# A Macaron block on one core: the first layer's expert rows added into three sums in HBM instead of two

## The chip, the core and the metric

The kernel runs on one core of one Trainium2 chip. The metric is device time in microseconds (us) from launch to end. A kernel's time here is the median of its runs. One further execution was taken with the hardware profiler, and all views of a profile come from that one.

Engines are called as in the profile: PE is TensorE's matmuls, PEld its weight loads, DVE is VectorE, ACT is ScalarE, POOL is GpSimd, SP is SyncE. SP computes nothing here; it issues DMAs. POOL, besides the constants at the start, issues the DMAs that gather, scatter or add.

## What is computed

The input is 4 sequences of 512 rows of 512 numbers, all float32. Three steps follow one another:

```
x = x + 0.5 * ffn(layernorm(x))
x = x + attention(layernorm(x))
x = x + 0.5 * ffn(layernorm(x))
```

`ffn` is a mixture of experts plus a shared expert. Each of the 2048 rows chooses 6 of 64 experts; an expert takes the rows that chose it, at most 96 of them, and computes `(silu(x @ w_gate) * (x @ w_up)) @ w_down` with a hidden size of 192. Its results, times the row's weight for that expert, are added to the row:

```
h = silu(einsum('ech,ehf->ecf', buf, w_gate)) * einsum('ech,ehf->ecf', buf, w_up)
out = einsum('ecf,efh->ech', h, w_down)
y = segment_sum(out[expert, slot] * w, token) + shared_expert(x)
```

So six expert results have to be added to each row, in float32. The two ffn steps use the same weights. The attention has 16 heads of 32, with rotary embedding.

## The kernel before, in words

**Stages.** From 0 to about 164 us the first layer's routing runs (row norms, choice of experts, lists of rows per expert), with the shared expert for three of the four sequences between its steps. From 164 to 458 us the first layer's expert loop runs (`experts(0, ...)`), then the attention for the four sequences in turn, whose pieces also do the second layer's routing. At about 1178 us the last sequence's routing follows, from 1229 us the second layer's expert loop, and at the end 16 DMAs add one sum to the output (line 1171).

**The expert loop** (`experts`, lines 531 to 608) goes over 32 pairs of experts. For pair n PE runs, in this order: the transposes of pair n+1's gathered rows (`turn`, line 547), the gate and up products of pair n (`hidden`, line 562, 96 matmul records), the down products of pair n-1 (`down`, line 577, 12 records). PE's order is written out by hand throughout.

- The rows of an expert are gathered by an indirect DMA that POOL issues (`load_rows`, line 538), into one of 11 buffers `xr`. A buffer is free again when the expert's results have been scaled, since the scale is read from it.
- The weights of a pair are three DMAs of 768 KB that SP issues (lines 262 to 264). There are six places for pairs, so those of pair n+6 go into the place of pair n once that is used up.
- The results of an expert stand in one of four PSUM banks (`eo`, pool psD). ACT scales them into a buffer `ob` (line 581; four buffers), and POOL issues an indirect DMA that adds its 96 rows into a sum in HBM (line 582). This is a scatter-add.
- Within the first layer, even experts add into `total[0][0]` and odd ones into `total[0][1]`. Two scatter-adds into the same sum may meet in a row, so each waits until the one before it into the same sum has landed. `total[0][0]` begins as the rows plus the shared expert's part (stored at line 528; for sequence 3, whose rows stay in SBUF, as zeros), `total[0][1]` as zeros (`clear`, line 235).

**From the loop to the attention.** In PSUM the loop's pools lie thus: psA, for the loop's turns, on banks 0 and 1; psB, for `gu`, on banks 2 and 3; psD, for `eo`, on banks 4 to 7. The attention opens psS (three tiles of two banks, banks 0 to 5) and then psT (banks 6 and 7). PE first runs the shared expert for the last sequence (lines 1068 to 1075), whose products go to psS tiles by the class `Banks`, and whose turns go to psT. Meanwhile the sums come back (`load`, line 614). For the first sequence SP loads the row tile of `total[0][0]` and that of `total[0][1]` (called `odd`), and DVE adds the two (line 808). For sequences 1 and 2 SP loads the one and POOL adds the other by an accumulating DMA (line 627). For sequence 3, which is in SBUF already, POOL adds both. The rows of sequence 1 are first read by the row statistics that DVE takes while the first sequence's projections run (`summed(1)`, line 1085; line 170). DVE's and ACT's orders are written out by hand here; POOL's and SP's orders are chosen by a scheduler when the program is made.

**The first 50 us.** SP's order is written out by hand: 16 loads of input rows (line 661) and three of shared weights, then for each of nine steps the store of the normed rows (line 309), read later by the gathers. `xn` has two buffers, so ACT's line 307 waits for the store two steps back.

Of the kernel before, what the change touches and what calls it, by code (L numbers as in the profile page):

```python
# [9 lines left out]
F32 = mybir.dt.float32  # L10
# [7 lines left out]
P = 128  # L18
B, S, D = 4, 512, 512
# [12 lines left out]
CAP = 96  # L32
# [51 lines left out]
def macaron_kernel(ctx: ExitStack, tc: tile.TileContext, X, ln_w, ln_b, W_in, W_out, gate_w, bias,  # L84
# [125 lines left out]
    def gate_up(bT, weights, rows, psum, pool, bufs):  # L210
# [8 lines left out]
        def products():  # L219
# [6 lines left out]

    xn_d = [dram.tile([T + P, XW], F32, tag=f"xn_d{i}", name=f"xn_d{i}") for i in range(2)]
    total = [[dram.tile([T + P, D], F32, tag=f"total{i}{j}", name=f"total{i}{j}") if (i, j) != (1, 0) else out  # L230
              for j in range(2)] for i in range(2)]

    def clear(layer, tiles):

# [31 lines left out]
    def load_now(*args):  # L266
        for go in load_pair(*args):
            go()
# [262 lines left out]
    def experts(layer, en, extra, psA, psB, psD, also):  # L531
        with ExitStack() as s:
            ep = s.enter_context(tc.tile_pool(name=f"ep{layer}", bufs=2))
            rows = {}

            def load_rows(e):
                xr = ep.tile([CAP, XW], F32, tag="xr", name="xr", bufs=GA + 5)
                nc.gpsimd.indirect_dma_start(  # L538
                    out=xr, out_offset=None, in_=xn_d[layer],
                    in_offset=bass.IndirectOffsetOnAxis(ap=en[:, e:e + 1], axis=0))  # L540
                rows[e] = xr

            bTs, hTs = {}, {}

            def turn(e):
                bTs[e] = ep.tile([P, DC, CAP], F32, tag="bT", name="bT", bufs=4)
                transposed(bTs[e], rows[e], DC, P, CAP, psA, nc.vector.tensor_copy)

            def hidden(n):


                wg, wu, _ = loaded[layer, n]
                xa, xb = bTs.pop(2 * n), bTs.pop(2 * n + 1)
                both = []
                for w in (wg, wu):
                    ps = psB.tile([P, 512], F32, tag="ps", name="gu")
                    both.append(ps[:, :3 * CAP])
                    g = both[-1].rearrange("p (k r) -> p k r", k=3)
                    for k in range(3):
                        for c in range(DC):  # L560
                            for t, x in enumerate((xa, xb)):
                                nc.tensor.matmul(g[t * FT:(t + 1) * FT, k, :], lhsT=w[:, t, c, k::3], rhs=x[:, c, :],  # L562
                                                 start=c == 0, stop=c == DC - 1)
                sg = ep.tile([P, 3 * CAP], F32, tag="sg", name="sg")
                hT = ep.tile([P, 3, CAP], F32, tag="hT", name="hT")
                nc.scalar.activation(sg, both[0], AF.Tanh, scale=0.5)  # L566
                nc.vector.scalar_tensor_tensor(sg, sg, 1.0, both[0], ALU.add, ALU.mult)  # L567
                nc.vector.tensor_mul(hT.rearrange("p k r -> p (k r)"), sg, both[1])
                hTs[n] = hT

            def down(n):
                wd, hT = loaded.pop((layer, n))[2], hTs.pop(n)
                eos = [psD.tile([P, 512], F32, tag="ps", name="eo") for _ in range(2)]
                for c in range(3):
                    for k in range(2):
                        r = slice(k * FT, (k + 1) * FT)
                        nc.tensor.matmul(eos[k][:CAP], lhsT=hT[r, c, :], rhs=wd[r, c, :], start=c == 0, stop=c == 2)  # L577
                for k in range(2):
                    e = 2 * n + k
                    ob = ep.tile([CAP, D], F32, tag="ob", name="ob", bufs=4)  # L580
                    nc.scalar.activation(ob, eos[k][:CAP], AF.Copy, scale=rows.pop(e)[:, D + e:D + e + 1])  # L581
                    nc.gpsimd.indirect_dma_start(  # L582
                        out=total[layer][k], in_=ob, in_offset=None,
                        out_offset=bass.IndirectOffsetOnAxis(ap=en[:, e:e + 1], axis=0),
                        compute_op=ALU.add, **(dict(bounds_check=T - 1, oob_is_err=False) if layer and not k else {}))

            for e in range(GA):
                load_rows(e)
            turn(0)
            turn(1)  # L590
            for n in range(E // 2 + 1):
                for e in range(2 * n + GA, min(2 * n + GA + 2, E)):
                    load_rows(e)
                if n + 1 < E // 2:
                    turn(2 * n + 2)
                    turn(2 * n + 3)
                if n < E // 2:
                    hidden(n)
                    if n + WS + WX + 1 < E // 2:
                        *gates, below = load_pair(layer, n + WS + WX + 1, extra)  # L600
                        for go in gates:
                            go()
                if n > 0:
                    down(n - 1)
                    for go in lasts:
                        go()
                lasts = [below] if n + WS + WX + 1 < E // 2 else []
                also(n)
# [5 lines left out]
    def load(b, i, op=None):  # L614

        rows = slice((b * TPB + i) * P, (b * TPB + i + 1) * P)
        if b < B - 1:
            x = row_tile(b * TPB + i)
            nc.sync.dma_start(x, total[0][0][rows, :])
            xas.setdefault(b, []).append(x)  # L620
        x = xas[b][i]
        if b == 0:
            odd = op.tile([P, 2, S], F32, tag="pT", name="odd")[:, 0, :]
            nc.sync.dma_start(odd, total[0][1][rows, :])
            return odd
        for k in range(1 if b < B - 1 else 0, 2):
            nc.gpsimd.dma_start(x, total[0][k][rows, :], accum_op=ALU.add, max_dma_last_dim=D)

    win, chunks = [], []
# [19 lines left out]
    with ExitStack() as s:  # L649
# [4 lines left out]
        with ExitStack() as f:  # L654
# [19 lines left out]
            for t in range(2 * TPB + 1):  # L674
                g, i = divmod(t, TPB)
                if t == TPB - 1:
                    with tc.issue_after(route.begun):
                        route.begin(1, xs[1])
                if g < 2:
                    route.row(g, xs[g], i)  # L680
                    route.turn(g, i)
                if t > 0:
                    route.score(*divmod(t - 1, TPB))
                if t == TPB:
                    for later in range(2, B):
                        with tc.issue_after(route.begun):
                            route.begin(later, xs[later])
                    route.choose(0)
# [61 lines left out]
    with ExitStack() as s:  # L750
# [2 lines left out]
        vp = s.enter_context(tc.tile_pool(name="vp", bufs=2))  # L753
        ap = s.enter_context(tc.tile_pool(name="ap", bufs=2))
        rp = s.enter_context(tc.tile_pool(name="rp1", bufs=1))
        psS = s.enter_context(tc.tile_pool(name="psS", bufs=3, space=bass.MemoryType.PSUM))
        psT = s.enter_context(tc.tile_pool(name="psT", bufs=2, space=bass.MemoryType.PSUM))
        s.enter_context(tc.manual_schedule(engines={mybir.EngineType.Activation, mybir.EngineType.DVE}))
        route = Route(1)
        route.use(rp, psT, psT, 2)  # L760
# [41 lines left out]
        def qkv(b):  # L802
# [2 lines left out]

            def row(i):
                if b == 0:
                    nc.vector.tensor_add(xs[b][i], xs[b][i], odds.pop(0))
                    if i + 2 < TPB:
                        odds.append(load(0, i + 2, op))  # L810
                    if i == 1:
                        load_win(3)
                        for later in range(1, B):
                            for k in range(TPB):
                                load(later, k)
                    for _ in first(b, row_stats(xs[b][i:i + 1]), (i,)):
                        pass
                while (b, i) not in stats:
                    work.flush(1)
                m, rr, _, _ = stats[b, i]  # L820
                lns[i] = ap.tile([P, D], F32, tag="row", name="ln", bufs=1)
                nc.vector.scalar_tensor_tensor(lns[i], xs[b][i], m, lnw_b, ALU.subtract, ALU.mult)
                nc.vector.scalar_tensor_tensor(lns[i], lns[i], rr, lnb_b, ALU.mult, ALU.add)
# [302 lines left out]
    with ExitStack() as s:  # L1126
        extra = s.enter_context(tc.tile_pool(name="wx1", bufs=WX))
        for n in range(WS, WS + WX):
            load_now(1, n, extra)
        psA = s.enter_context(tc.tile_pool(name="psA1", bufs=2, space=bass.MemoryType.PSUM))  # L1130
        psB = s.enter_context(tc.tile_pool(name="psB1", bufs=2, space=bass.MemoryType.PSUM))
        psD = s.enter_context(tc.tile_pool(name="psD1", bufs=4, space=bass.MemoryType.PSUM))
        with ExitStack() as f:
            g = B - 1
# [75 lines left out]
```

## Time and profile before

| what | us |
|---|---|
| median of 3 runs | 1554.72 (1552.41 to 1554.78) |
| time of the profiled execution | 1552.3 |
| its span, first to last instruction | 1550.6 |
| first gather of the first loop issued | 150.1 |
| first `hidden` matmul, pair 0 | 164.5 |
| the same, pair 31 | 434.4 |
| last scatter-add of the first loop issued | 457.3 |
| first `hidden` matmul of the second loop | 1229.5 |

| engine | busy us, share of the span |
|---|---|
| PE | 1358.0 (88%) |
| PEld | 774.0 (50%) |
| DVE | 628.8 (41%) |
| ACT | 596.9 (38%) |
| POOL | 350.7 (23%) |

How to read it: the chain of waits starts at the last instruction and goes back, at each step, to what released it. A line such as "DMA total<-ob,en" in it is a scatter-add that somebody waited for. "issue" is time for which the profile shows no reason. A line of the list of instructions ends, in square brackets, with the idle time of the engine before it and what ended that. A row of a stretch's busy times has the granted TensorE clock (1.00 is full speed), the busy share of the DMA engines and the bytes that they moved. That share adds up the packets of all queues, which overlap, so that it can exceed 1. Engine totals mix stages with different limits; what a change in one stage is worth has to be read in that stage.

### The profile page before, as it was taken

The page shows a single profiled execution, that of the slowest core. Times are in us where ns is not written, and L with a number is a line of the kernel's source. Part 1 is how long each engine was busy: PE and PEld are TensorE (multiplying, and loading weights), DVE is VectorE, ACT ScalarE, POOL GpSimd, SP SyncE. Part 2 cuts the span into 40 slices and gives each one's busy share as a digit, 9 for nine tenths or more (in the row PEclk, how much of TensorE's full clock was granted, in tenths as well). Part 3 has the DMA queues.
Part 4 walks back from the last instruction along what each step waited for, and adds up shares of the span by engine and source line. Part 5 has one row for each costly group of instructions (what it writes and reads, how often), then busy time and mean ns, then how long its engine had stood idle before and what let it go on. Part 6 is the DMA issues. An engine that isn't in the chain of part 4 may idle for free.

```text
span 1550.6 us, 27673 instructions
## 1 busy us (share of the span) xinstructions
PE 1358.0 (88%) x11328; PEld 774.0 (50%) x11328; DVE 628.8 (41%) x1572; ACT 596.9 (38%) x1161; POOL 350.7 (23%) x321
## 2 busy tenths in 40 slices
PE   4785899988978998999999999998898899989890
PEld 4553676766643443334443334334344577766660
DVE  7575222221216576257333862375515522222210
ACT  4431121211111377667645785557462121111120
POOL 2001455554435000000000000000000255555455
PEclk9898899999989997999899999996998999999995
DMA  5367999999979210000000001000205699999959
GB/s 198 133 229 264 313 322 323 323 328 336 327 210 184 63 68 1 1 1 0 21 21 18 1 16 74 11 14 34 92 1 209 198 335 332 337 332 322 331 127 124
DMA packets 110717, 254.86 MB, mean 164 GB/s; under 512 B 15848, under 2 KB 32360, under 8 KB 110592
## 3 DMA queue, kind: packets, MB, share of 16 engines
q1 hardware_dynamic: 70880, 192.96, 35.4%
q0 software_dynamic: 39424, 59.97, 18.8%
q8 instruction: 90, 1.47, 0.4%
q14 instruction: 35, 0.29, 0.1%
q10 hardware_dynamic: 288, 0.16, 0.0%
HBM read 202.21 MB, written 56.95 MB: 167 GB/s over the span
## 4 chain that ended last, share of the span: by engine, by line
PE 42%; DMA 30%; issue 7%; ACT 5%; DVE 4%; POOL 2%; SPq 0%; POOLq 0%; ACTq 0%; DVEq 0%
DMA total<-ob,en 19%; PE pq L834 10%; DMA out_dram<-ob,en 9%; PE sct L1018 5%; PE sc L988 4%; PE cx L1041 4%; PE sct L1022 4%; PE po L883 3%; PE gu L214 3%; PE so L520 3%; DMA xr<-xn_d,en 2%; PE ps_t L207 2%; ACT sc L996 2%; PE lg L320 1%; POOL out_dram L1171 1%
## 5 line engine op out<-in xcount | busy, mean ns | idle before, releaser
L538 POOL DMA_INDIRECT xr<-xn_d,en x128 | 119.6, 934 | 883.6 <-DVE sg L221 711.8
L562 PE MATMUL gu<-bT,w 128*64 128x96 f32 x6144 | 296.9, 258 | 0.0
L562 PEld LDWEIGHTS gu<-bT,w 128*64 128x64 f32 x6144 | 286.4, 175 | 8.7 <-issue 1.8
L581 ACT ACTIVATE ob<-eo,xr 96x512 f32<-96x512 f32 x128 | 85.7, 682 | 409.8 <-PE eo L577 187.6
L996 ACT ACTIVATE sc<-sc,nmq 128x512 f32<-128x512 f32 x256 | 168.9, 660 | 56.0 <-DVE nmq L991 50.4
L834 PE MATMUL pq<-w,lT 128*128 128x512 f32 x384 | 179.3, 614 | 6.2 <-ACT lT L208 2.7
L991 DVE TENSOR_REDUCE nmq<-sc 128x2 f32<-128x1024 f32 x128 | 151.5, 1221 | 76.1 <-PE sc L988 76.0
L582 POOL DMA_INDIRECT total<-ob,en x96 | 138.5, 1443 | 186.2 <-DMA total<-ob,en 143.6
L577 PE MATMUL eo<-w,hT 64*96 64x512 f32 x768 | 180.0, 602 | 0.0
L208 DVE COPY bT<-ps_t 128x384 f32<-128x384 f32 x128 | 68.6, 555 | 209.6 <-PE ps_t L207 209.6
L1029 ACT ACTIVATE pT<-sct 128x1024 f32<-128x1024 f32 x128 | 124.1, 1022 | 61.8 <-PE sct L1022 61.8
L834 PEld LDWEIGHTS pq<-w,lT 128*128 128x128 f32 x384 | 71.5, 195 | 96.8 <-issue 81.0
L207 PE MATMUL ps_t<-ident,xr 96*128 96x96 f32 x512 | 64.2, 258 | 56.7 <-DMA xr<-xn_d,en 39.4
L214 PE MATMUL gu<-wsgu,xT 128*128 128x384 f32 x256 | 97.2, 528 | 8.4 <-ACT ob L581 8.1
L567 DVE SCALAR_TENSOR_TENSOR sg<-sg,gu 128x288 f32<-128x288 f32 x64 | 29.1, 455 | 181.6 <-ACT sg L566 181.6
L207 PEld LDWEIGHTS ps_t<-ident,xr 96*128 96x128 f32 x512 | 46.8, 143 | 109.1 <-issue 80.7
L988 PE MATMUL sc<-kT,qT 32*128 32x512 f32 x512 | 94.6, 706 | 7.0 <-ACT sc L996 6.3
L1018 PE MATMUL sct<-qT,kT 32*128 32x512 f32 x512 | 94.6, 661 | 2.8 <-ACT pT L1029 2.7
L577 PEld LDWEIGHTS eo<-w,hT 64*96 64x96 f32 x768 | 58.7, 159 | 74.1 <-issue 68.3
L1022 PE MATMUL sct<-nmT,pick 4*128 4x512 f32 x512 | 86.7, 604 | 0.0
L214 PEld LDWEIGHTS gu<-wsgu,xT 128*128 128x128 f32 x256 | 52.0, 209 | 50.5 <-issue 18.3
L1041 PE MATMUL cx<-pT,v 128*32 128x512 f32 x512 | 73.5, 630 | 0.5 <-DVE acc L470 0.5
(163 smaller groups left out, 1317.5 us busy)
## 6 DMA issues: line engine op xcount, KB each, us to landing
w<-in_L_ffn_w_gate_dram SPq DMA_DIRECT2D x64, 768.0 KB, 21.4
w<-in_L_ffn_w_up_dram SPq DMA_DIRECT2D x64, 768.0 KB, 21.8
w<-in_L_ffn_w_down_dram SPq DMA_DIRECT2D x64, 768.0 KB, 21.6
total<-zero SPq DMA_DIRECT2D x39, 256.0 KB, 4.7
xn_d<-xn SPq DMA_DIRECT2D x32, 256.0 KB, 2.0
out_dram<-total POOLq DMA_DIRECT2D x16, 256.0 KB, 10.9
x<-total POOLq DMA_DIRECT2D x11, 256.0 KB, 10.2
shelf<-in_L_attn_X_dram SPq DMA_DIRECT2D x9, 256.0 KB, 7.2
```

Of the source, the lines that this page charges most:

```text
L207: nc.tensor.transpose(view[:, c, :], src[:, c * w:(c + 1) * w], ident[:rows, :rows])
L214: nc.tensor.matmul(gu[:rows, :2 * F].rearrange("p (w f) -> p w f", w=2), lhsT=bT[:, c, :], rhs=weights[:, :, c, :], start=c == 0, stop=c = ...
L562: nc.tensor.matmul(g[t * FT:(t + 1) * FT, k, :], lhsT=w[:, t, c, k::3], rhs=x[:, c, :], start=c == 0, stop=c == DC - 1)
L577: nc.tensor.matmul(eos[k][:CAP], lhsT=hT[r, c, :], rhs=wd[r, c, :], start=c == 0, stop=c == 2)
L582: nc.gpsimd.indirect_dma_start(out=total[layer][k], in_=ob, in_offset=None, out_offset=bass.IndirectOffsetOnAxis(ap=en[:, e:e + 1], axis=0 ...
L834: nc.tensor.matmul(pq, lhsT=lTs[i][:, c, :], rhs=win[n][c], start=c == 0, stop=c == DC - 1)
L988: nc.tensor.matmul(scs[j // 2][:, j % 2, :], lhsT=qT[b][rows, c, q * P:(q + 1) * P], rhs=kT[b][rows, c, :], start=True, stop=True)
L991: nc.vector.tensor_reduce(nmv[:, q, 2 * pair:2 * pair + 2, c], scs[pair], AX.X, ALU.max, negate=True)
L996: nc.scalar.activation(scs[j // 2][:, j % 2, :], scs[j // 2][:, j % 2, :], AF.Exp, bias=nmq[:, q, j * DH + c:j * DH + c + 1], accum_out=sm ...
L1018: nc.tensor.matmul(scs[j // 2][:, j % 2, :], lhsT=kT[b][rows, c, kt * P:(kt + 1) * P], rhs=qT[b][rows, c, :], start=True, stop=False)
L1022: nc.tensor.matmul(scs[j // 2][:, j % 2, :], lhsT=pick[rows, c, :], rhs=nmT[b][c // (NC - 1)][rows, :], start=False, stop=True)
L1041: nc.tensor.matmul(cx[c][j * DH:(j + 1) * DH, :], lhsT=v[b][:, kt, h * DH:(h + 1) * DH], rhs=pTs[j // 2][:, j % 2, :], start=kt == 0, stop ...
```

## The change

1. The first layer's scatter-adds go into three sums by `e % 3`. A third tensor `total[0][2]` is cleared by 17 DMAs of 256 KB, two in each of the nine steps at the start, ahead of the step's store of normed rows.
2. Reading back: for the first sequence SP loads two `odd` tiles for each row tile and DVE adds twice; for the others POOL issues one more accumulating DMA for each row tile.
3. `ob` has five buffers instead of four, in both layers' loops.
4. The attention's psT is opened ahead of psS, so it takes banks 0 and 1, and psS banks 2 to 7. In the last stage psB1 is opened ahead of psA1.

```
     total = [[dram.tile([T + P, D], F32, tag=f"total{i}{j}", name=f"total{i}{j}") if (i, j) != (1, 0) else out
-              for j in range(2)] for i in range(2)]
+              for j in range(3 - i)] for i in range(2)]
...
-                    ob = ep.tile([CAP, D], F32, tag="ob", name="ob", bufs=4)
+                    ob = ep.tile([CAP, D], F32, tag="ob", name="ob", bufs=5)
                     nc.scalar.activation(ob, eos[k][:CAP], AF.Copy, scale=rows.pop(e)[:, D + e:D + e + 1])
                     nc.gpsimd.indirect_dma_start(
-                        out=total[layer][k], in_=ob, in_offset=None,
+                        out=total[layer][e % (3 - layer)], in_=ob, in_offset=None,
...
-            odd = op.tile([P, 2, S], F32, tag="pT", name="odd")[:, 0, :]
-            nc.sync.dma_start(odd, total[0][1][rows, :])
+            odd = op.tile([P, 2, S], F32, tag="pT", name="odd")
+            for k in (1, 2):
+                nc.sync.dma_start(odd[:, k - 1, :], total[0][k][rows, :])
             return odd
-        for k in range(1 if b < B - 1 else 0, 2):
+        for k in range(1 if b < B - 1 else 0, 3):
             nc.gpsimd.dma_start(x, total[0][k][rows, :], accum_op=ALU.add, max_dma_last_dim=D)
...
+                for k in range(2 * t, min(2 * t + 2, NT + 1)):
+                    nc.sync.dma_start(total[0][2][k * P:(k + 1) * P, :], zero[:, :D])
                 if g < 2:
                     route.row(g, xs[g], i)
...
+        psT = s.enter_context(tc.tile_pool(name="psT", bufs=2, space=bass.MemoryType.PSUM))
         psS = s.enter_context(tc.tile_pool(name="psS", bufs=3, space=bass.MemoryType.PSUM))
-        psT = s.enter_context(tc.tile_pool(name="psT", bufs=2, space=bass.MemoryType.PSUM))
...
-                    nc.vector.tensor_add(xs[b][i], xs[b][i], odds.pop(0))
+                    odd = odds.pop(0)
+                    for k in range(2):
+                        nc.vector.tensor_add(xs[b][i], xs[b][i], odd[:, k, :])
...
+        psB = s.enter_context(tc.tile_pool(name="psB1", bufs=2, space=bass.MemoryType.PSUM))
         psA = s.enter_context(tc.tile_pool(name="psA1", bufs=2, space=bass.MemoryType.PSUM))
-        psB = s.enter_context(tc.tile_pool(name="psB1", bufs=2, space=bass.MemoryType.PSUM))
```

## The prediction

> **What bounds the kernel now.** I read the page first, the chain that ended last above all, then the chain over the first expert loop, the sums by stretch around its end, the instructions there in order of time, and the read-back of the sums.
>
> ```profile
> PE 42%; DMA 30%; issue 7%; ACT 5%; DVE 4%; POOL 2%; SPq 0%; POOLq 0%; ACTq 0%; DVEq 0%
> DMA total<-ob,en 19%; PE pq L834 10%; DMA out_dram<-ob,en 9%; PE sct L1018 5%; PE sc L988 4%; PE cx L1041 4%; PE sct L1022 4%; PE po L883 3%; PE gu L214 3%; PE so L520 3%; DMA xr<-xn_d,en 2%; PE ps_t L207 2%; ACT sc L996 2%; PE lg L320 1%; POOL out_dram L1171 1%
> ```
>
> The largest item is the scatter-add. The same chain over part of the first loop, in order of time:
>
> ```profile
> 268.58 0.52 issue
> 269.10 0.02 POOLq L538
> 269.12 0.19 issue
> 269.31 8.32 DMA total<-ob,en
> 277.63 0.02 issue
> ```
>
> One scatter-add into a sum lands after 8.3 us, 0.8 us go by, and the next into that sum is issued: 9.1 to 9.2 us for each pair, since each sum gets one expert of a pair. PE would need 8.0: pairs 1 to 8, before the four `ob` buffers are used up, start 8.0 us apart (171.1 to 227.1 us). Pairs 8 to 31 start on average 9.0 apart (227.1 to 434.4). The end of the loop, by stretch and by instruction:
>
> ```profile
> core 0: us, PE busy (x) PEld busy (x) DVE busy (x) ACT busy (x) POOL busy (x), PEclk, DMA share, GB/s
> 187.00:440.00 253.00, 234.64 (x3344) 174.29 (x3344) 55.45 (x112) 48.69 (x87) 127.26 (x106) 0.99 1.05 328
> 445.00:452.00 7.00, 0.00 (x0) 0.00 (x0) 0.00 (x0) 1.66 (x3) 2.81 (x2) 0.68 0.50 68
> 452.00:460.00 8.00, 7.56 (x15) 4.21 (x16) 0.71 (x2) 0.72 (x2) 4.21 (x3) 0.64 0.59 73
> ```
>
> ```profile
> 451.71 0.68 ACT L581 ACTIVATE ob<-eo,xr 96x512 f32<-96x512 f32 x1 [3.06 <-DMA total<-ob,en]
> 452.44 8.05 PE L214 MATMUL gu<-wsgu,xT 128*128 128x384 f32 x16 [8.09 <-ACT ob L581]
> ...
> 468.67 2.75 PE L214 MATMUL gu<-wsgu,xT 128*128 128x384 f32 x8
> ...
> 474.94 0.68 DVE L808 TENSOR_TENSOR shelf<-shelf,odd 128x512 f32<-128x512 f32 x1
> ...
> 480.27 0.75 DVE L823 SCALAR_TENSOR_TENSOR ln<-ln,rs,lnb_b 128x512 f32<-128x512 f32 x1
> ```
>
> PE's last `eo` ends at 444.36. It then stands for 8.09 us: the next matmul needs PSUM that the last `ob` (451.71 to 452.39) frees, and that one waited for a scatter-add to free its buffer. Then 16 matmuls take 8.05 us where 8 later take 2.75. DMA is close to full through the loop (328 GB/s, share 1.05), a second limit just behind the first.
>
> **The third sum and the fifth buffer.** With three sums, an expert's scatter-add waits for the one three before: 3 in 9.2 us, 6.1 us for a pair, under PE's 8.0. This holds only if a landing stays near 8.3 us with more in flight. The page "DMA: Bandwidth & Descriptors" of the Trainium skill (section "Anatomy of one DMA") speaks against it: a fixed cost of about 2.0 us, mostly the receipt of the last write, the rest data movement. By that, some 6 of the 8.3 us would be occupied DMA engines, and a third scatter-add in flight would only lengthen the queue; the loop would gain nothing. The packets in the trace decide: 96 of 2048 bytes belong to each scatter-add, and put to the issues in order they start 5.1 us after the issue and go on until 7.1, for nearly every one from pair 10 to 25. Landing follows about 1 us later. So only 2.0 of 8.3 us are movement; the rest is delay that overlaps. I take the trace. The gathers' packets take 1.6 us of the same queue, so a pair needs 2 x 2.0 + 2 x 1.6 = 7.2 us of it, which fits into 8.0, though narrowly.
>
> Next late are the weights. SP's queue works in order, so counting its bytes tells when each load was in: the up weights of pair 12 at 232.5, used at 262.4; of pair 20 at 314.7, used at 334.8; of pair 31 at 423.3, used at 434.4. The lead shrinks from 29.9 to 11.1 us. A faster loop uses it up and then runs at the pace of the loads, whatever PE could do. Earlier scatter-adds also come in the loads' way: in half microseconds full of scatter packets SP's queue moved 193 GB/s, without any from POOL's queue 339. One costs the loads 2.0 x (339 - 193) / 339 = 0.86 us. At 423 us the scatter-adds up to pair 26 were through; PE at the loads' heels needs about 6 more by then: 5.2 us. So pair 31's weights come at 428.5, and its first matmul moves from 434.4 to there: **-5.9**. (Bounds: -11.1 if the extra traffic costs nothing; 0 if it costs the whole lead.)
>
> From there PE has 9.9 us of matmuls (434.44 to 444.36). Then only the two last `ob` remain, as after pair 0, whose second ended 1.3 us after its `eo`. With five buffers the last `ob` needs the scatter-add five before, issued some 10 us earlier. The stop of 8.1 us becomes 1.3: **-6.8** (0 if a wait for a landing stays).
>
> The short stop should also save the slow start. "TensorE: Matmul & The Clock Gate" (Part 1) says an idle window of about 3.4 us halves the clock. Here 0.68 and 0.64 were granted over 445 to 460, and the 16 matmuls cost 8.05 - 2 x 2.65 = 2.75 us more than at full clock. After 1.3 us idle I count this as gone: **-2.7** (0 if the clock drops anyway).
>
> **The fifth buffer in the second loop: 0.** It is paced by its two sums as before (8.0 to 8.7 us landings in its chain), whatever waits ahead of them. Bounds: -4 (an expert's pace) to +1.
>
> **The changed banks: 0.** PE's first matmul after the loop writes bank 0, yet waits for the last `ob`, whose bank is 6: a pool waits for all of every pool it overlaps. psS on banks 2 to 7 overlaps psD as it did on 0 to 5, and the first matmul is still in psS. In the last stage the scores come up to 1.7 us sooner (they waited for DVE L885), but the next ones wait for DVE's statistics of the last row. Bounds: -1.5 to +0.5.
>
> **Clearing the third sum.** 17 DMAs of 256 KB at the start; over 20 to 60 us the DMA share is below a third, which hides 15 of them. The first two pairs stand in SP's queue ahead of the first two stores of `xn`, whose first landing (22.07) already ends a 1.9 us wait of ACT L307. Two more DMAs at 0.65 us, the pace of SP's issues there: **+1.3**, on PE's row of transposes and scores. Bounds: 0 to +3.
>
> **Reading back.** DVE's second add is 0.68 us for each of four rows. The first lies on the path (L808 to L823 to PE); the fourth as well, since PE waits for its `ln` at 518.43; the two others have over 4 us of slack: **+1.4**. The eight SP loads instead of four (0.43 us to issue) lie under the shared expert's 25 us of PE work, with the rows needed 12 us after the last landing; without that cover they would cost about 3 us.
>
> POOL issues 28 accumulating DMAs instead of 16:
>
> ```profile
> L627 POOL DMA_DIRECT2D x<-total x11: 1268/1847/5985, 465.9 to 503.2; - x11
> L627 POOL DMA_DIRECT2D shelf<-total x5: 1283/2373/3497, 470.9 to 479.3; - x5
>   DMA x<-total: 13.8, 3
>   DMA shelf<-total: 3.7, 1
> ```
>
> The 16 took from 466 to about 508, 2.65 us each; 28 will take 75. The second add to a row waits for the first (median landing 8.8), and POOL's later DMAs queue behind that wait. DVE reads sequence 1's rows (L170) at 503.9 to 509.7, where their adds landed by about 490. Everything shifts by some 13 us, so the reads come at 491 to 497, and POOL can start at about 453. If sequence 1's eight adds are among the first 14, they land by 453 + 14 x 2.65 = 490: no cost. If spread to the 20th place, 506: 9 us of DVE standing still, and behind it the rotary products and PE. I take **+2**, near the first, since POOL's present order puts sequence 1 in places 2 and 4 to 6. Bounds 0 and +9. Sequences 2 and 3 are read at 617 and later: hidden.
>
> **Sum.** -5.9 - 6.8 - 2.7 + 1.3 + 1.4 + 2 = -10.7. Against the profiled 1552.3 (span 1550.6 and 1.7 around it) that gives 1541.6. The runs' median, 1554.72, lies 2.4 above the profiled time; from it 1544.0.
>
> **Rivals.**
> *The weights' queue is the whole bound* (0.15): pair 31 stays at 434.4 and only the tail gains: -6.8 - 2.7 + 4.7 = -4.8, 1550. For it: 1.05 and 328 GB/s throughout. Against: 11.1 us of lead left.
> *The third sum only queues* (0.07): a landing grows to 3 x 9.2 / 2 = 13.8 us, pace and stop stay, and the added work remains: +3 to +5, 1558. For it: POOL's queue would be full for 7.2 of 8.0 us. Against: the packets.
> *The rows of sequence 1 come late* (0.16), the case that ends slower: POOL's order takes the adds of all rows once before second ones. If sequence 1's last is in place n, it lands at 453 + 2.65 n, against 497. The other terms gain 12.7, so it decides from n = 22 on; at n = 24 the wait is 20 us: +7, 1562. For it: the adds take turns on the DMA engines anyway. Against: the present order.
> *The change does not do what it says*: for the banks I assume just that (0 above). If the pool's wait were for its own banks only, 1.3 us more would be gained.
>
> **How the numbers follow.** The likeliest case (0.62) gives 1544, by itself 1537 to 1551. A change within 0.2% (3.1 us), about what a measurement of this kernel can tell from none, needs terms of two cases at their ends. Faster: the likeliest case nearly whole and most of the second: 0.73. Slower: the third and most of the fourth: 0.17. Within: 0.10. Range 1536 to 1559: at its low end the loads cost nothing extra and the adds are in time, at its high end the adds are late.
>
> **What would show it.** Right: in the first loop ACT no longer waits for landings before `ob`; three scatter-adds are in flight, landing in 8 to 10 us; pair 31 starts at 426 to 431, now behind its weights; PE's stop after the loop is under 2 us and L214's first 16 matmuls take about 5.4. Wrong: landings of 12 us or more, or a long DVE wait at L170 for POOL's adds between 490 and 520.

## The result, and the profile after

The changed kernel takes 1558.92 us (median of 22 runs, 1552.51 to 1569.77), the kernel before in the same series 1554.62 (22 runs, 1546.55 to 1564.64): ratio 1.0040, 95% interval 1.0023 to 1.0058. It is 0.4% slower; the forecast was 1544.0 us, 0.7% faster. The profiled execution took 1555.39 us, with a span of 1553.7. That 1558.9 still lies inside the stated range of 1536 to 1559 is luck: the range's high end was meant for rows of sequence 1 that come late, and they did not.

The chain of waits of the changed kernel, by engine and by line:

```profile
PE 48%; DMA 9%; ACT 5%; DVE 4%; issue 3%; POOL 1%; POOLq 0%; DVEq 0%; ACTq 0%
PE pq L840 10%; DMA out_dram<-ob,en 8%; PE sct L1024 5%; PE gu L563 5%; PE sc L994 4%; PE cx L1047 4%; PE sct L1028 4%; PE po L889 3%; PE gu L214 3%; PE ps_t L207 3%; PE so L521 3%; PE eo L578 2%; ACT sc L1002 2%; PE lg L321 1%; DMA xr<-xn_d,en 1%
```

The scatter-adds of the first layer, 19% of the chain before, are gone from it, and PE's own gate and up products (`gu L563`) are in it instead. What ScalarE waited for in the first loop, before (187 to 453 us) and changed (187 to 450 us); columns are total, times, longest, in us:

```profile
ACT ob L581 <- DMA total<-ob,en: 90.7, 29, 5.7
```

```profile
ACT ob L582 <- PE eo L578: 144.4, 29, 5.2
```

So the third sum does what it says: no scaled rows wait for a landing any more. The stretches of the first loop and of its end in the changed kernel, and PE's and ACT's instructions at that end:

```profile
187.00:440.00 253.00, 242.94 (x3352) 178.43 (x3350) 54.97 (x114) 47.65 (x86) 132.72 (x111) 1.00 1.05 329
445.00:452.00 7.00, 5.61 (x25) 2.26 (x22) 0.00 (x0) 2.51 (x4) 3.77 (x3) 1.00 1.04 291
```

```profile
449.24 1.26 ACT L582 ACTIVATE ob<-eo,xr 96x512 f32<-96x512 f32 x2 [1.32 <-issue]
```

```profile
450.55 5.43 PE L214 MATMUL gu<-wsgu,xT 128*128 128x384 f32 x16 [1.39 <-ACT ob L582]
```

The stop behind the loop is 1.39 us (8.09 before), and its 16 matmuls take 5.43 us (8.05 before), as forecast. Yet the loop holds 242.94 us of PE work for 3352 matmuls where it held 234.64 for 3344: they take longer. Where the two profiles differ (us; the experiments show below that they come from two kinds of chip):

| stretch | before | changed | difference |
|---|---|---|---|
| start to pair 0's first matmul | 164.5 | 170.9 | +6.4 |
| from there to pair 31's | 269.9 | 268.4 | -1.5 |
| pair 31 to the last `eo` | 9.9 | 9.8 | -0.1 |
| stop behind the loop | 8.1 | 1.4 | -6.7 |
| from there to attention's first projection | 30.0 | 28.8 | -1.2 |
| to the second loop's first gather | 733.8 | 737.7 | +3.9 |
| to pair 32's first matmul | 13.2 | 15.4 | +2.2 |
| to the end | 321.1 | 321.2 | +0.1 |

**The start.** ScalarE's instructions in the changed kernel, then in the kernel before (start, duration, what):

```profile
30.58 1.26 ACT L308 ACTIVATE xn<-shelf,off,rs 128x512 f32<-128x512 f32 x1
33.04 0.58 ACT L208 COPY xT<-ps_t 128x512 f32<-128x512 f32 x1 [1.20 <-PE ps_t L207]
34.64 0.22 ACT L326 ACTIVATE lgs<-lg 128x64 f32<-128x64 f32 x1 [1.01 <-PE lg L321]
34.76 1.28 ACT L308 ACTIVATE xn<-shelf,off,rs 128x512 f32<-128x512 f32 x1
```

```profile
28.83 1.26 ACT L307 ACTIVATE xn<-shelf,off,rs 128x512 f32<-128x512 f32 x1
29.89 0.62 ACT L208 COPY xT<-ps_t 128x512 f32<-128x512 f32 x1
31.16 0.22 ACT L325 ACTIVATE lgs<-lg 128x64 f32<-128x64 f32 x1 [0.64 <-PE lg L320]
32.01 0.59 ACT L208 COPY xT<-ps_t 128x512 f32<-128x512 f32 x1 [0.63 <-PE ps_t L207]
33.61 0.23 ACT L325 ACTIVATE lgs<-lg 128x64 f32<-128x64 f32 x1 [1.01 <-PE lg L320]
33.73 2.31 ACT L307 ACTIVATE xn<-shelf,off,rs 128x512 f32<-128x512 f32 x2
```

Before, a row is normed (`xn`) ahead of the copies of the row before it. In the changed kernel each row goes alone: norm, transpose, copy, score, then the next norm, 4.2 us a row, and PE waits for each `xn`. Nothing wrote this order by hand: here only SP's and PE's orders are, and the scheduler that makes the program (the planner, in what follows) places ACT's and DVE's instructions. The waits of ACT for a store of normed rows, from 20 to 46 us, before and changed:

```profile
ACT xn L307 <- DMA xn_d<-xn: 1.9, 1, 1.9
```

```profile
ACT xn L308 <- DMA xn_d<-xn: 3.2, 1, 3.2
```

The zeros in front of the stores thus cost ACT the 1.3 us that were forecast; the rest of its delay is not a wait for a store. The tenth row is stored at 50.33 us instead of 43.37, the first weights are asked for at 69.91 instead of 63.83.

**The loop.** PE and then POOL in pair 14 of the changed kernel:

```profile
290.90 4.54 PE L563 MATMUL gu<-bT,w 128*64 128x96 f32 x91
295.66 0.51 PE L563 MATMUL gu<-bT,w 128*64 128x96 f32 x5 [0.22 <-issue]
```

```profile
291.20 1.45 POOL L583 DMA_INDIRECT total<-ob,en  x1 [3.11 <-ACT ob L582]
292.95 0.94 POOL L539 DMA_INDIRECT xr<-xn_d,en  x1 [0.30 <-issue]
294.19 1.45 POOL L583 DMA_INDIRECT total<-ob,en  x1 [0.30 <-DMA total<-ob,en]
```

Of 96 matmuls, 91 have begun when PE starts no other for some 0.5 us (0.22 of it without any running); it goes on at 295.66, where POOL's third issue ends (295.64). Pairs 2 to 28 nearly all have this, at the same place against POOL. It is POOL's place that counts, not PE's: in pair 10 POOL's issues stand some 0.36 us earlier in the block, and PE stops after 84 matmuls instead of 91:

```profile
255.81 4.12 PE L563 MATMUL gu<-bT,w 128*64 128x96 f32 x84
260.20 0.82 PE L563 MATMUL gu<-bT,w 128*64 128x96 f32 x12 [0.28 <-issue]
```

```profile
258.74 1.45 POOL L583 DMA_INDIRECT total<-ob,en  x1 [0.30 <-issue]
```

Nor do the loads of the program's own instructions explain it: they come about once a pair too, but end anywhere from 0.1 to 5.3 us from the stop. The blocks of pairs 2 to 28 last 5.2 us instead of 4.50 and pairs start 8.7 to 8.8 us apart instead of 8.0.

### The profile page after: what moved, and what is told of

It is laid out like the page before. It is cut to its first block, busy times and chain, and to the rows that moved or that the text cites. A ratio compares the mean times of both kernels' runs of the same rounds, so it can differ in the third digit from the quotient of the medians.

```text
span 1553.7 us, 27718 instructions
## 1 busy us (share of the span) xinstructions
PE 1366.2 (88%) x11328; PEld 777.1 (50%) x11328; DVE 630.1 (41%) x1576; ACT 594.7 (38%) x1161; POOL 365.8 (24%) x333
## 4 chain that ended last, share of the span: by engine, by line
PE 48%; DMA 9%; ACT 5%; DVE 4%; issue 3%; POOL 1%; POOLq 0%; DVEq 0%; ACTq 0%
PE pq L840 10%; DMA out_dram<-ob,en 8%; PE sct L1024 5%; PE gu L563 5%; PE sc L994 4%; PE cx L1047 4%; PE sct L1028 4%; PE po L889 3%; PE gu L214 3%; PE ps_t L207 3%; PE so L521 3%; PE eo L578 2%; ACT sc L1002 2%; PE lg L321 1%; DMA xr<-xn_d,en 1%
## 5 line engine op out<-in xcount | busy, mean ns | idle before, releaser
L563 PE MATMUL gu<-bT,w 128*64 128x96 f32 x6144 | 310.1, 257 | 14.3 <-issue 11.5
L563 PEld LDWEIGHTS gu<-bT,w 128*64 128x64 f32 x6144 | 291.5, 173 | 31.2 <-issue 20.9
L582 ACT ACTIVATE ob<-eo,xr 96x512 f32<-96x512 f32 x128 | 80.7, 678 | 294.2 <-PE eo L578 286.4
L567 ACT ACTIVATE sg<-gu 128x288 f32<-128x288 f32 x64 | 26.3, 411 | 195.8 <-PE gu L563 173.9
L207 PE MATMUL ps_t<-ident,xr 96*128 96x96 f32 x512 | 60.0, 257 | 35.8 <-DMA xr<-xn_d,en 33.0
L569 DVE TENSOR_TENSOR hT<-sg,gu 128x288 f32<-128x288 f32 x64 | 29.1, 454 | 129.9 <-PE gu L563 127.6
```

Of the source, the lines that this page charges most:

```text
L207: nc.tensor.transpose(view[:, c, :], src[:, c * w:(c + 1) * w], ident[:rows, :rows])
```

## Experiments

Theories at the outset. A: the zeros at the start cost more than forecast, and PE's gap comes with POOL's issues, which follow each other directly now that none waits for a landing. B: the gap comes with where the fifth buffer or the pools put things. C: the pools cost time in the last stage. The runs went to four chips, called P (e1 to e4), Q (e5 to e8), R (e9 to e12) and S (e13 to e18). Each timed run stands beside 17 to 35 runs of the kernel before on its own chip. The table has the profiled executions; "0 to 31" is pair 0's first matmul to pair 31's.

| run | chip | ratio, 95% interval | first gather | 0 to 31 | stop | PE's gap |
|---|---|---|---|---|---|---|
| e1 | P | 0.9994 (0.9961-1.0027) | 160.2 | 267.8 | 1.4 | no |
| e2 | P | 0.9989 (0.9959-1.0019) | 147.4 | 273.9 | 3.3 | no |
| e3 | P | 0.9997 (0.9960-1.0034) | 149.2 | 275.4 | 3.6 | no |
| e4 | P | 0.9988 (0.9949-1.0028) | 148.2 | 267.3 | 1.4 | no |
| e5 | Q | 1.0049 (1.0021-1.0077) | 154.4 | 271.4 | 1.4 | yes |
| e6 | Q | 1.0008 (0.9977-1.0039) | 155.4 | 271.7 | 1.4 | yes |
| e9 | R | 0.9988 (0.9954-1.0023) | 152.4 | 271.9 | 1.4 | yes |
| e10 | R | 1.0636 (1.0586-1.0686) | 152.9 | 369.0 | 1.4 | second loop |
| e13 | S | 0.9968 (0.9933-1.0003) | 151.2 | 268.7 | 1.4 | no |
| e14 | S | 0.9971 (0.9942-0.9999) | 151.6 | 269.4 | 1.4 | no |
| e17 | S | 0.9975 (0.9957-0.9993) | 151.3 | 268.5 | 1.4 | no |
| e18 | S | 0.9943 (0.9910-0.9977) | 151.1 | 266.1 | 1.4 | no |

**e1, e2, e3: the parts alone.** e1 is the third sum with its clears; e2 only `bufs=5` for `ob`; e3 only the pools:

```
-        psS = ...; psT = ...                 +        psT = ...; psS = ...
-        psA = ... "psA1"; psB = ... "psB1"   +        psB = ... "psB1"; psA = ... "psA1"
```

> Only the third sum is added to the kernel before; four buffers of expert rows, PSUM pools in the old order. Theory A (GpSimd now issues scatter, gather, scatter with 0.3 us between them, since no scatter waits for a landing any more, and TensorE stands still at the end of such a chain): the gate and up blocks of pairs 2 to 28 stay at 5.2 us (4.50 before) with the one gap of 0.5 us, first rows are gathered some 5 us late, and the time is that of the whole change, 1556 to 1561 us. Theory B (the gap comes with where the fifth buffer or the swapped pools put things): the blocks are 4.50 us, the loop is limited by the weights, and the time is 1551 to 1556 us.

> Only the fifth buffer of expert rows is added to the kernel before. Theory A: no block of pairs 2 to 28 is longer than in the kernel before (4.50 us, 6.0 where the clock is halved), and the time is within 0.2% of it, 1551.5 to 1557.7 us. Theory B: blocks show a gap of 0.5 us wherever GpSimd issues scatter, gather, scatter with 0.3 us between them, also in the second loop, and the time is 1555 to 1560 us.

> Only the order of the PSUM pools is changed, in attention and in the last stage. Theory A: nothing (1551.5 to 1557.7 us): the first matmul of attention's stage still waits for the last scaled expert rows, 8 us behind the loop. Theory C (the last stage, between the last scores and the second loop's first gather, is 5 to 6 us longer in the changed kernel because its pools now share banks with attention's other turns): that stretch is 211 to 212 us instead of 206 and the time is 1559 to 1561 us.

Measured: e1 1553.66, e2 1550.69, e3 1551.77 us, beside 1551.92 of the kernel before. The fifth buffer and the pools are worth nothing that shows within 0.4%; C falls (208.7 us for its stretch in e3, and 207.2 in e4, which has the swapped pools too; 206.2 before, 206.4 in e1). In e1 ScalarE has the changed kernel's order at the start, and the first gather comes at 160.2 us: the clears make it, not the other parts. But e1 shows no gap, with the same issues of POOL. PE, then POOL, in e1:

```profile
287.59 4.50 PE L563 MATMUL gu<-bT,w 128*64 128x96 f32 x96
```

```profile
287.89 1.45 POOL L583 DMA_INDIRECT total<-ob,en  x1 [2.31 <-ACT ob L582]
289.64 0.94 POOL L539 DMA_INDIRECT xr<-xn_d,en  x1 [0.30 <-issue]
290.88 1.45 POOL L583 DMA_INDIRECT total<-ob,en  x1 [0.30 <-issue]
```

The issues stand at 0.30, 2.05 and 3.29 us behind the block's start, to 0.01 us as in the changed kernel's pair 14, and all 96 matmuls run in 4.50 us. Against A as it was stated: the issues alone are not enough.

**e4, e6: the clears behind the rows.** e4 is the whole change, e6 the third sum alone, each with:

```
-                for k in range(2 * t, min(2 * t + 2, NT + 1)):
-                    nc.sync.dma_start(total[0][2][k * P:(k + 1) * P, :], zero[:, :D])
...
+            for k in range(NT + 1):
+                nc.sync.dma_start(total[0][2][k * P:(k + 1) * P, :], zero[:, :D])
             rest = [go for n in (0, 1, 2, 4, 5) for go in load_pair(0, n, extra)]
```

> The whole change, but the 17 clears of the third sum are issued behind the store of the eighth row of tokens, not two by two between the first nine. Theory A (the 4.4 MB of zeros stand in SyncE's queue in front of the rows' stores, and ScalarE's next row waits for a store to land): the eighth row's store is issued at 43.5 us as in the kernel before (50.3 in the changed one), the first gather at 150 to 151 us (155.0), and, since the weights start 6 us earlier and set the end of the first loop, the time falls by 4 to 6 us to 1553 to 1555 us. Rival (TensorE's gaps set the loop, or the zeros cost the same wherever they stand): the first gather or the last pair stays where it is in the changed kernel, and the time is 1557 to 1560 us.

> The third sum alone, with its clears behind the eighth row's store; four buffers of expert rows and the old pools. If the buffer and the pools are worth nothing, this is the run with all parts and the clears moved: first gather at 148 to 151 us, a stop of 1.4 us behind the first loop, 1545 to 1551 us, 3 to 8 us below the three sums with their clears in front of the rows. If the fifth buffer or the pools made that run's gain, the stop behind the loop is 3 us or more and the time is within 0.2% of before.

Measured: e4 1550.53 us (before: 1551.92), e6 1555.70 (before: 1554.09, changed 1562.03 on the same chip). So e6 takes 6.3 us less than the changed kernel on chip Q, though not the 1545 to 1551 that were expected. Its profile does not show where: that execution took 1564.79 us, and its first pair starts at 171.6, no earlier than e5's (170.8). The start is not mended in it: the planner has a third order here, rows 9 and 10 are stored at 47.5 and 48.1 us in e6 (41.7 and 43.4 before), and the first gather comes at 155.4. That e4 has it at 148.2 goes with PE: its short matmuls left their slow pace at 28 us, in e6 between 41 and 46 (last section).

**e5, e7, e8: the changed kernel again, and less weights.** e5 has no edit. e7 is the kernel before and e8 is e4's, both with a third of each `w_down` loaded from pair 7 on, so that part of the result is left out (one execution each, as for the other versions with less weights):

```
+        part = 1 if layer == 0 and n > 6 else 3
-                lambda: nc.sync.dma_start(wd, w_down[two]...)]
+                lambda: nc.sync.dma_start(wd[:, :part], w_down[two]...[:, :part])]
```

> The changed kernel as it stands, beside the others. In its first profile TensorE stood still for 0.5 us near the end of the gate and up block in pairs 2 to 28 (blocks of 5.2 us instead of 4.50), and neither the three sums alone nor the whole change with the clears moved showed that under the same issues of GpSimd. If the gap belongs to this program, the blocks are 5.2 us here too and the time is 1555 to 1560 us (0.3% above before); if it belongs to that one execution or chip, the blocks are 4.50 us, TensorE waits for weights around pair 21 instead, the last pair starts where it did (439 to 445 us), and the time is 1552 to 1557 us.

> The kernel before with less to load: from pair 7 of the first loop on, only the first of w_down's three chunks is loaded (0.26 MB of 0.79) and stands in for the other two, so two thirds of those w_downs are left out of the result. A pair brings 1.84 MB of weights instead of 2.36. If the scatters' landings set the first loop, pair 31's first matmul stays within 5 us of 434; if the weights do as well, it comes 5 to 15 us earlier (landings get shorter too when the queues carry less). Never below 164.5 + 31 x 8.0 = 412.

> The whole change with the clears moved, and the same two thirds of w_down left out from pair 7 of the first loop on. If the weights' supply is what keeps the third sum's gain in the loop, no pair waits for weights any more, pairs come every 8.0 us and pair 31's first matmul is at 410 to 415 us instead of 432.5: the third sum is then worth 10 to 20 us against the kernel before with the same weights. If something else limits the loop (GpSimd, the rows), it stays at 425 or later.

Measured: e5 1562.03 us (before: 1554.09), with the gap. e7 takes 1534.05 us, 264.3 from pair 0 to 31, which starts at 429.6 (434.4 before); e8 1570.60 and 270.3. On this chip e6 and e8 have the gap too, and so has e7, the kernel before with two sums, where its issues meet. In e7 the two kinds of pair stand in one execution. Pair 5, then pair 9, each time PE and POOL's third issue:

```profile
206.26 4.53 PE L563 MATMUL gu<-bT,w 128*64 128x96 f32 x92
211.08 0.43 PE L563 MATMUL gu<-bT,w 128*64 128x96 f32 x4 [0.29 <-issue]
```

```profile
209.56 1.45 POOL L583 DMA_INDIRECT total<-ob,en  x1 [0.30 <-issue]
```

```profile
241.48 4.50 PE L563 MATMUL gu<-bT,w 128*64 128x96 f32 x96
```

```profile
245.25 1.45 POOL L583 DMA_INDIRECT total<-ob,en  x1 [0.32 <-issue]
```

In pair 5 the end of the third issue (211.01) falls into the block, and PE stops; in pair 9 it comes 0.7 us behind the block, which runs in 4.50 us. So the gap belongs neither to a part of the change nor to one execution: it goes with the chip, and on it with POOL's third issue. B falls. e8 answers its question otherwise than meant: with few weights the loop still takes 8.7 us a pair, with the gap in nearly every pair and no wait for weights.

To see what goes with it I counted, in all profiles with both loops, POOL's issues whose last 0.5 us fall into a gate and up block, by their place in a row (a break under 0.4 us counts as no break). In the changed kernel's profile and e5 to e12, PE stopped at the end of 214 of 230 third issues in a row, and of 3 of 904 first or second ones; by a like count, a fourth in a row stopped it in 2 of 83. In the kernel before, e1 to e4, e13, e14, e17 and e18 it did at none of 120 third ones (in the kernel before alone these are only some eight). The profile of the kernel before thus comes from a chip without the gap and that of the changed kernel, which is one of the 22 timed runs, from one with it; their loops can't be compared directly.

**e9, e10: the clears beside the others.** e9 is the whole change, with each clear issued beside the second sum's:

```
-            more = [lambda t=t: clear(0, (t,)) for t in range(NT + 1)]
+            more = [lambda t=t: (clear(0, (t,)), nc.sync.dma_start(total[0][2][t * P:(t + 1) * P, :], zero[:, :D]))
+                    for t in range(NT + 1)]
```

e10 adds POOL's order written out and pauses: scatter, gather, three memsets, scatter, three memsets, gather.

> The whole change, but each clear of the third sum is issued right beside the clear of the second sum that is already spread over 64 to 150 us, where the DMA engines are some 70% busy, instead of between the first nine rows. If the start's loss comes from zeros ahead of the row stores (rows later, TensorE idle and longer at its slow start, and the planner's other order for VectorE and ScalarE), the first rows are stored and the eighth row's transpose runs as in the kernel before, and the first gather is at 148 to 152 us (154 to 160 with the clears between the rows); 3 to 8 us under the changed kernel: 1551 to 1556 us. If 4.4 MB more cost the same anywhere, the gather is at 154 us or later.

> The same, with GpSimd's order in the first loop written out and three small memsets (some 0.5 us) between a gather and the next scatter and between a scatter and the next gather, so that no three indirect DMAs are issued back to back. If the chain of three is what stops TensorE for 0.5 us: on a chip that shows the gap in the run beside this one, the gate and up blocks of pairs 2 to 28 fall from 5.2 to 4.5 us and pairs come every 8.0 us until weights run short, the time 2 to 6 us lower; on a chip without the gap nothing changes (within 0.2%). If the gap stays with the pauses, it has another cause.

Measured: e9 1556.51 us (before: 1557.21). ACT's order at the start is the old one, row for row: what PE waited for from 20 to 52 us in e9, and in the changed kernel,

```profile
PE ps_t L207 <- ACT xn L308: 5.0, 2, 3.6
```

```profile
PE ps_t L207 <- ACT xn L308: 10.9, 6, 4.8
```

The tenth row is stored at 41.6 us and the first gather issued at 152.4. e10, at 1659.08 us, is a failed experiment: I had written the gathers three experts later than the planner has them, and PE waited for rows (first loop of e10):

```profile
PE ps_t L207 <- DMA xr<-xn_d,en: 91.7, 22, 7.0
```

Its third issues fell behind the blocks, so it tells nothing of the gap.

**e11, e12: less weights, without and with these pauses.** e11 is e8's kernel, e12 adds e10's order.

> The whole change with the clears behind the rows and two thirds of w_down left out from pair 7 of the first loop on, once more, as the partner of the next run. On a chip with TensorE's gap: 8.7 us per pair. On one without: 8.0 us per pair, no wait for weights, pair 31's first matmul 246 to 250 us behind pair 0's (267 with all weights).

> The same with less of w_down, and with the pauses in GpSimd's chain. If back to back issues make the gap and nothing else limits the loop, pairs come every 8.0 to 8.1 us on either kind of chip, pair 31's first matmul 246 to 252 us behind pair 0's; if the gap has another cause, as the run beside it on a chip that shows the gap (270 us).

Measured: e11 1554.44 us, 264.2 from pair 0 to 31; e12 1647.87, failed as e10. What PE waited for in e11's first loop, whole:

```profile
PE gu L564 <- issue: 7.2, 27, 0.3
```

No weights, no rows, only the gap, once a pair.

**e13 to e18: the order put right.** e14 and e18 are e9 with POOL's order written out as the planner had it, gathers nine and ten experts ahead; e13 and e17 add one memset at each of two places; e15 and e16 are e8's kernel, with less weights and the clears behind the rows, with this order and with (e15) or without (e16) the memsets.

```
+                        if k:
+                            nc.gpsimd.memset(idle, 0.0)
+                        if gathers:
+                            load_rows(gathers.pop(0))
+                        if not k:
+                            nc.gpsimd.memset(idle, 0.0)
```

> The whole change with the third sum's clears beside the second's; GpSimd's order in the first loop written out as the planner had it (scatter, gather, scatter, gather, the gathers nine and ten rows ahead), and one memset (0.2 us, which with its start makes a break of some 0.75 us) between gather and second scatter and between second scatter and second gather. If three issues back to back make TensorE's gap: blocks of pairs 2 to 28 at 4.5 us, 8.0 us per pair until the weights run short, and 2 to 5 us under the run without the pauses; 1549 to 1554 us, under both kernels. If the gap has another cause: blocks of 5.2 us as in the run beside this. On the one kind of chip that showed no gap, both are equal.

> The same written order without the memsets. Blocks of 5.2 us with the gap of 0.5 us on a chip that shows it, 8.7 us per pair, 1552 to 1557 us as with the planner's own order (1556.5 against 1557.2 for the kernel before on that chip).

> The clears behind the rows, two thirds of w_down left out from pair 7 of the first loop on, the written order and the memsets. If the row of three makes the gap, 8.0 to 8.1 us per pair and pair 31's first matmul 246 to 251 us behind pair 0's; otherwise 264 to 270 us as in the runs without pauses.

> The same without the memsets: 264 to 270 us from pair 0 to pair 31 on a chip with the gap, 246 to 251 us on one without.

> The written order with the memset between gather and second scatter and between second scatter and second gather. On a chip whose run without the memsets shows the gap: no gap and blocks of 4.5 us if the row of three causes it, pairs every 8.0 us until weights run short, 2 to 6 us under the other run; blocks of 5.2 us if it has another cause. On a chip without the gap: as the other run, some 0.3% under the kernel before.

> The same without the memsets. On a chip with the gap: blocks of 5.2 us, 8.7 us per pair, within 0.2% of the kernel before. On one without: 4.5 us, 8.0 us per pair up to the weights' wait at pair 21, 0.3% under the kernel before.

Measured: e13 1550.72, e14 1551.95 (before: 1554.27); e17 1549.95, e18 1544.91 (before: 1552.70); e15 1530.34, e16 1531.55 us. All six ran on chip S, which has no gap, so the pause was not tried where it matters: whether it removes the gap stays open. What S shows is the third sum without the gap. What PE waited for in the first loop of e14 (all weights), and the stretches of e14 and e16:

```profile
PE gu L565 <- DMA w<-in_L_ffn_w_gate_dram: 17.0, 2, 10.0
PE gu L565 <- DMA w<-in_L_ffn_w_up_dram: 2.3, 2, 1.6
```

```profile
187.00:400.00 213.00, 196.91 (x2804) 145.71 (x2802) 47.73 (x99) 41.36 (x74) 119.18 (x101) 0.97 1.05 327
```

```profile
187.00:400.00 213.00, 213.00 (x3118) 159.31 (x3119) 51.92 (x108) 44.39 (x80) 127.92 (x107) 1.00 1.05 320
```

In e14 pairs start every 8.0 us up to pair 20; then the weights' lead is used up and pair 21 comes 20 us behind pair 20. In e16, with fewer weights, PE works through the whole stretch: 245.9 us from pair 0 to 31 against 269.4. So without the gap, the weights' supply is what holds the loop of three sums at 269 us and not at 246. These four timed versions came out 0.3 to 0.6% under the kernel before on their chip (the interval of e13 alone takes in no change). They were not run beside the changed kernel, nor on a chip with the gap.

## Why the prediction was wrong, step by step

- **Clearing the third sum, +1.3, bounds 0 to +3: the step that failed.** Pair 0's first matmul came 6.4 us later in the profile. Beside runs with two sums on the same chip it is 5.5 us later on Q (170.8 in e5, 165.3 in e7) and about 12 on P (177.0 in e1, 164.0 and 165.1 in e2 and e3). I counted two DMAs in SP's queue and found the engines free. That part came as counted: ACT waited 1.3 us longer for a store. At nothing, and without a reason, stood what the DMAs do to the order: the planner gave ACT another one, row by row, and PE waited 10.9 us for `xn` from 20 to 52 us instead of 5.0. In all three profiles with the clears between the rows ACT has this order. e9 changes only the place of the clears: ACT's order is the old one again and pair 0 starts at 167.9 (166.4 to 167.1 in e13, e14, e17, e18). Clears behind the rows give the third order and 165.2 to 174.4 (e4, e6, e8, e11, e15, e16). No run keeps the old order with the clears between the rows, and why the planner chooses another (it may reckon the stores late behind the zeros) was argued, not shown.
- **The loop, -5.9.** Measured -1.5 in the profile. The mechanism was right where there is no gap: the lead is used up and weights set the end. Two sums need 269.9, 273.9 and 275.4 us from pair 0 to 31 (before, e2, e3; mean 273.1), three 266.1 to 269.4 (e1, e4, e13, e14, e17, e18; mean 268.0): -5.1. Where there is one, three need 268.4 to 271.9 (changed, e5, e6, e9; mean 270.9): 2.9 us more. Two sums with all weights have no profile on such a chip, so what the third is worth there is not shown. The step took 8.0 us for PE's pace from pairs 1 to 8 of a chip without the gap, where three issues in a row (pairs 2, 3 and 7 have them) cost nothing. It also read the lead high: where the trace tells when a weight load landed, from 200 us on, that is 2.3 to 4.9 us after its last byte was counted.
- **The stop, -6.8**: -6.7 in the profile. But 8.1 us was high: e2 and e3, with two sums, have 3.3 and 3.6, so on the average of these three it is -3.6. **The slow start, -2.7**: the 16 matmuls gained 2.6.
- **DVE's adds, +1.4**: right as to the path, and a little low. The first row's add takes 1.41 us instead of 0.68:

```profile
470.42 1.41 DVE L814 TENSOR_TENSOR shelf<-shelf,odd 128x512 f32<-128x512 f32 x2
477.57 1.08 PE L207 MATMUL ps_t<-ident,ln 128*128 128x128 f32 x4 [5.09 <-issue]
```

  For the fourth row, PE's 16 projections ahead of it take 8.0 us from start to start in all four profiles with two sums and 8.8 to 9.3 in all with three (9.2 changed). Of the 2.6 us gained ahead of attention's first projection, 1.2 are left: 0.7 go to the first row's add, 0.5 to the transposes behind it (1.08 us at a granted clock of 0.50, 0.63 at 0.71 before; e2 and e3, with two sums, have 1.09), 0.2 to a slower small instruction of DVE.
- **Late rows of sequence 1, +2**: 0; from attention's first projection to that of sequence 1 it is 56.2 us before and 55.8 changed, and DVE waited for no add there. POOL issued the 28 adds in 53 us, 1.9 each instead of the 2.65 reckoned.
- **Fifth buffer, 0, and banks, 0**: e2 and e3, right within 0.4%.
- **No term at all** was given to what follows. From the first projection to the second loop's first gather it took 3.9 us more; the profiles with two sums have 733.1 to 737.9 us there, those with three 730.7 to 748.7. The stretch behind the last sequence's scores alone is 6.1 us longer, and its length goes with the granted clock: 123.3 us at 0.94 before and 129.4 at 0.89 changed, also 129.3 at 0.89 in e8, but 123.6 to 126.1 at 0.93 to 0.95 in e1, e4, e5 and e6. Whether the third sum has a share in it stays open. The 2.2 us ahead of pair 32 are the chip's: 15.4 to 17.8 us on Q and R, also in e7 with two sums, 12.8 to 13.4 on P and S.

The forecast was -10.7 and the profiles differ by +3.1. Of these 13.8 us, 5.1 arose at the start, 4.4 in the loop and 6.1 in the two stretches without a term; the read-back and the matmuls after the stop came out 1.9 better. The sign seems to hang on the chip, though the changed kernel itself was not timed on one without the gap: the two series in which the changed kernel is slower (1.0040, and 1.0049 in e5) ran on chips with the gap, while e1, with the same clears and the latest start of all, equals the kernel before on a chip without it (0.9994), and so does e9, with the start mostly mended, on one with it (0.9988).

Of the rivals, the one that ends slower (late rows) did not happen: the result was slower for reasons that no case held. "The weights' queue is the whole bound" was half true: the weights set the end of the loop on chips without the gap, but the third sum still gained some 5 us there.

## What to carry to other kernels

Added DMAs are costed by what they do to the order too: where a planner places an engine's instructions, compare that engine's order with the old one, before any queue is counted. When a wait is removed, list what the waiting engine will now do without a break, and who runs beside it. Before two profiles are compared stretch by stretch, find out whether they come from the same chip: a run of both kernels on one chip told more here than two profiles.

## What the runs showed of the hardware

- On two of four chips, and on that of the changed kernel's profile, TensorE starts no matmul in the last 0.5 us of GpSimd's third indirect DMA in a row, without waiting for any semaphore (214 of 230 cases); on the two others never (0 of 120), with the same issues to 0.01 us. Why it is the third issue, and what tells the chips apart, is open.
- TensorE's transposes of normed rows in the first 42 us of the kernel before take 421 ns, those after 54 us 273 ns (min, median, max in ns):

```profile
L207 PE MATMUL ps_t<-ident,xn x26: 421/421/477, 17.7 to 38.2; 128*128 128x128 f32 x26
...
L207 PE MATMUL ps_t<-ident,xn x16: 272/273/273, 57.8 to 90.0; 128*128 128x128 f32 x16
```

The granted clock reads 1.00 from 20 to 60 us, over both paces. "TensorE: Matmul & The Clock Gate" (Part 1) of the Trainium skill has TensorE start slow until it has been busy for a window; the durations agree with a slow start, but the column of the granted clock does not show it here. The slow pace ended between 42 and 46 us before and, with a row every 4.2 us, between 48 and 53 in the changed kernel; in e4's profile it ended at 28, for a reason that no run tests.
